# Factors by root and reciprocal, the skip in the segment's number, whole-block searches, and earlier norms of heads in a graph-attention kernel

## The chip, the cores and the metric

The kernel runs on one core of one Trainium2 chip. The metric is the device time in microseconds. Before the change the median of three runs is 234.67 us (234.59 to 234.72). Beside them stands one profiled execution of 234.5 us, whose recorded span is 233.0 us.

## The reference

One layer of graph attention over 4096 nodes with 512 features and 4 heads, a residual, and a layer norm:

```python
ht = (h @ W).reshape(N, 4, 512).transpose(1, 0, 2)
src, dst = einsum('hnd,hd->hn', ht, a_src), einsum('hnd,hd->hn', ht, a_dst)
e = leaky_relu(src[:, :, None] + dst[:, None, :], 0.01) + adj[None]
att = softmax(e, axis=-1)
x = layernorm(x + einsum('hij,hjd->hid', att, ht).mean(axis=0))   # eps 1e-5
```

Here h is x (4096x512, fp32), adj is 4096x4096 in fp32, W is 512x2048 and a holds two vectors of 512 for each head. The entries of adj are zero, or positive numbers up to 1e9. The scores from src and dst are small beside them, so in a row whose two largest entries lie far enough apart the softmax is one at the largest entry, in all four heads. Then the row of the attention result is x at that column, times the mean of the four W.

## The kernel before, in words

The kernel works by that. For each row it finds the column of the largest entry of adj, gathers the row of x of that column (y), multiplies it by the mean of the heads' W (w_sum), adds the row's own x, and normalises. In the end it tests for each row, with bounds from the norms of W, a and x, that the second largest entry is far enough below. Only where a row fails does a general path run (the function general).

The rows are cut into 32 blocks of 128. The main loop runs over turns t = 0 to 31. All engines take their instructions in the order in which the program lists them, since the schedule is written out by hand (manual_schedule). A turn works on several blocks at once:

- SyncE issues the load of the adj tile of block t + 5 (2 MB, a ring of six tiles; it waits until the search of block t - 1 has let go of its tile) and, every fourth turn, a load of rows of x.
- VectorE searches tile t (segment_maxima: the largest entry of each segment of 16, 32 or 64 columns, in two halves of 2048 columns; then find_segment: the largest of these and its index), and finds the column of block t - 2 (find_column). In most turns up to 19 (the tuple END) the column comes after the segment, later between the two halves of the search.
- GpSimd computes the row numbers for an indirect gather of the winning segment (fetch_segment, tile lead) and for the gather of the rows of x (gather_rows, tile y).
- TensorE transposes the gathered rows of block t - 3 (turn) and multiplies them by w_sum (products). For blocks 1 to 17 (TABLED) rows of x below number 128 are not gathered. GpSimd adds SKIP (8192) to their number, which puts it out of bounds, the gather leaves the cleared tile as it is, and the row comes from a small table through a one-hot matrix (spread, from_table).
- ScalarE makes that one-hot matrix (Square, then Relu), copies the transposed rows (yt), sums squares of W and x, and takes the mean and the sum of squared deviations of block t - 4 (parked_stats, at the end of its turn); it applies the norm of block t - 9 (finish).

Every fourth turn from 8 to 28, rstd turns four blocks' sums into factors 1/sqrt(var + eps). In the kernel before GpSimd does all of it: a scaling, a power with exponent -0.5, a product for the shift and a scaling. GpSimd's order in such a turn is: row and lead of block t, then the column and the gather of block t - 2, then rstd. head_norms has three parts, in turns 24, 26 and 28; its middle part is the first Sqrt on ScalarE.

Lines that matter: segment_maxima L196 to L206, find_segment L208, fetch_segment L216, gather_rows L236, find_column L259, spread L322, parked_stats L359, rstd L365, finish L372, head_norms L453, and the loop L523 to L584, with this in it:

```python
COLUMN, PROJECT, STATS, FINISH = 2, 3, 4, 8
END = (*range(1, 3), *range(5, 20))
...
    if t >= FINISH and t % Q == 0:
        rstd(slice(t - FINISH, t - FINISH + Q))
```

Behind the loop the last blocks are projected and normalised, the norms and the test are completed, and the finished rows are stored.

Of the kernel before, what the change touches and what calls it, by code (L numbers as in the profile page):

```python
# [9 lines left out]
F32 = mybir.dt.float32  # L10
BF16 = mybir.dt.bfloat16
U32 = mybir.dt.uint32
I32 = mybir.dt.int32
AF = mybir.ActivationFunctionType
OP = mybir.AluOpType
# [3 lines left out]
EPS = 1e-5  # L19
LOWEST = -3.4028234663852886e38  # L20
HINTED = tuple(getattr(mybir.EngineType, name) for name in ("PE", "Activation", "DVE", "Pool"))
P = 128
# [6 lines left out]
SKIP = 8192  # L29
# [43 lines left out]
def leading_rows(ctx, tc, x, adj, W, a, out, ident, n_bad, any_bad):  # L73
# [8 lines left out]
    nc = tc.nc  # L82
# [35 lines left out]
    def pieces(ib):  # L118
        return PIECES if ib == NB - 1 else 2 if ib >= LATE else 1
# [45 lines left out]
    width = once.tile([P, len(spans)], U32, name="width")  # L165
    for k, (e, _, _) in enumerate(spans):
        nc.gpsimd.iota(width[:, k : k + 1], pattern=[[0, 1]], base=e, channel_multiplier=0)
    power = once.tile([P, 4], F32, name="power")
    nc.gpsimd.memset(power, -0.5)
    eps = once.tile([P, 1], F32, name="eps")  # L170
    nc.gpsimd.memset(eps, EPS)
    zero = once.tile([P, 1], F32, name="zero")
    nc.gpsimd.memset(zero, 0.0)
    nth = once.tile([P, 1], I32, name="nth")
    nc.gpsimd.iota(nth, pattern=[[0, 1]], base=0, channel_multiplier=-1)
    minus = once.tile([P, 1], F32, name="minus")
    nc.gpsimd.tensor_copy(minus, nth)
    ident_b = once.tile([P, P], BF16, name="ident_b")
# [17 lines left out]
    def segment_maxima(ib, lo, hi):  # L196

        e = spans[span_of(ib)][0]
        if lo == 0:
            seg_of[ib] = small.tile([P, N // e], F32, name=f"seg{e}", bufs=2)  # L200
        n = max(pieces(ib), 2)
        for k in range(lo * n // PIECES, hi * n // PIECES):
            nc.vector.tensor_reduce(  # L203
                seg_of[ib][:, ts(k, N // e // n)],
                adj_t[ib][:, ts(k, N // n)].rearrange("p (s e) -> p s e", e=e), axis=AX.X, op=OP.max,
            )  # L206
# [9 lines left out]
    def fetch_segment(ib):  # L216
        at = at_of.pop(ib)
        row = small.tile([P, 1], U32, name="row")
        nc.gpsimd.tensor_tensor(row, at[:, 0:1], first[:, ib : ib + 1], op=OP.add)  # L219
        k = span_of(ib)  # L220
        e = spans[k][0]
        lead = lead_pool.tile([P, e], F32, name=f"lead{e}", bufs=LEADS[k])
        nc.gpsimd.indirect_dma_start(  # L223
            out=lead, out_offset=None, in_=adj_segs[e],
            in_offset=bass.IndirectOffsetOnAxis(ap=row[:, :1], axis=0),
        )
        lead_of[ib] = lead
        if ib < NB - 1:
            start = at_of[ib] = small.tile([P, 1], U32, name="start")
            nc.gpsimd.tensor_tensor(start, at[:, 0:1], width[:, k : k + 1], op=OP.mult)  # L230

    def clear_rows(ib):
        y = y_t[ib] = y_pool.tile([P, D], F32, name="y")
# [2 lines left out]
    def gather_rows(ib, col):  # L236
        if ib not in TABLED:
            y = y_t[ib] = y_pool.tile([P, D], F32, name="y")
            nc.gpsimd.indirect_dma_start(  # L239
                out=y, out_offset=None, in_=x,  # L240
                in_offset=bass.IndirectOffsetOnAxis(ap=col[:, :1], axis=0),
            )
            return
        away = small.tile([P, 1], U32, name="away")
        nc.gpsimd.tensor_scalar(away, col, float(P), float(SKIP), op0=OP.is_lt, op1=OP.mult)
        there = small.tile([P, 1], U32, name="there")
        nc.gpsimd.tensor_tensor(there, col, away, op=OP.add)  # L247
        nc.gpsimd.indirect_dma_start(  # L248
            out=y_t[ib], out_offset=None, in_=x,
            in_offset=bass.IndirectOffsetOnAxis(ap=there[:, :1], axis=0),  # L250
            bounds_check=N - 1, oob_is_err=False,
        )
        low = low_of[ib] = small.tile([P, 1], BF16, name="low")
        nc.gpsimd.tensor_scalar(low, col, float(P), None, op0=OP.min)

    def find_inner(ib):
        nc.vector.max(out=inner[:, ib, :], in_=lead_of[ib])
# [94 lines left out]
    def stats(ib):  # L352
        o, i = o_ps[ib], slice(ib, ib + 1)
        sq = rows.tile([P, D], F32, name="sq")
        nc.scalar.activation(sq, o, AF.Identity, scale=-1.0 / D, accum_out=nm[:, i])
        sq = rows.tile([P, D], F32, name="sq")
        nc.scalar.activation(sq, o, AF.Square, bias=nm[:, i], accum_out=sd[:, i])

    def parked_stats(ib):  # L359
        o, i = o_ps.pop(ib), slice(ib, ib + 1)  # L360
        nc.scalar.activation(hold[:, ib, :], o, AF.Identity, scale=-1.0 / D, accum_out=nm[:, i])  # L361
        sq = rows.tile([P, D], F32, name="sq")
        nc.scalar.activation(sq, hold[:, ib, :], AF.Square, bias=nm[:, i], scale=-float(D), accum_out=sd[:, i])  # L363

    def rstd(i):  # L365
        nc.gpsimd.tensor_scalar(sd[:, i], sd[:, i], 1.0 / D, EPS, op0=OP.mult, op1=OP.add)
        nc.gpsimd.tensor_tensor(sd[:, i], sd[:, i], power[:, : i.stop - i.start], op=OP.pow)  # L367
        nc.gpsimd.tensor_mul(nm[:, i], nm[:, i], sd[:, i])
        if i.stop <= BEHIND:
            nc.gpsimd.tensor_scalar(sd[:, i], sd[:, i], -float(D), None, op0=OP.mult)  # L370
# [82 lines left out]
    def head_norms(part):  # L453

        if part == 0:
            each = once.tile([2 * H, 2 * H], F32, name="each")
            nc.vector.tensor_scalar_mul(each, ident[: 2 * H, : 2 * H], aa)
            pw = of_norms[0] = psum.tile([P, KB * H + 2 * H], F32, name="px", bufs=1)
            nc.tensor.matmul(pw[:, : KB * H], ones, ww, start=True, stop=True)
            nc.tensor.matmul(pw[:, KB * H :], ones[: 2 * H, :], each, start=True, stop=True)  # L460
        elif part == 1:
            pw = of_norms[0]
            w2 = once.tile([P, H], F32, name="w2")
            nc.vector.tensor_reduce(
                w2, pw[:, : KB * H].rearrange("p (k h) -> p h k", h=H), axis=AX.X, op=OP.add
            )
            for s in range(2):
                nc.vector.tensor_mul(n2[:, ts(s, H)], pw[:, ds(KB * H + s * H, H)], w2)
            nc.scalar.activation(n2, n2, AF.Sqrt)
        else:  # L470
            both = once.tile([P, H], F32, name="both")
            nc.vector.tensor_add(both, n2[:, :H], n2[:, H:])
            nc.vector.tensor_reduce(vn, both, axis=AX.X, op=OP.max)
# [44 lines left out]
    squares = list(range(KB * H))  # L518
    squares_at = {t: 2 if t < 7 else 1 for t in range(3, 15)}
    COLUMN, PROJECT, STATS, FINISH = 2, 3, 4, 8  # L520
    END = (*range(1, 3), *range(5, 20))

    for t in range(NB):  # L523
        if t == NB // 2:
            tc.mark_branch_hint_location("general", engines=HINTED)
        if t in x_at:
            load_x(*x_at[t])
        if t + AHEAD == NB - 1:
            load_x(LATE, Q)
        load_adj(t + AHEAD)  # L530
        middle = 1 if t == NB - 1 else 2
        segment_maxima(t, 0, middle)
        if t >= COLUMN and t not in END and t != COLUMN + 1:
            find_column(t - COLUMN)
        segment_maxima(t, middle, PIECES)
        if t == NB - 1:
            for ib in (BEHIND, BEHIND + 2):
                load_x(ib, 2)
        find_segment(t)
        if t in END:  # L540
            find_column(t - 1 if t <= COLUMN else t - COLUMN)
        if t + 1 in TABLED:
            clear_rows(t + 1)
        if t >= FINISH and t % Q == 0:
            rstd(slice(t - FINISH, t - FINISH + Q))
        if t < 2:
            mean_of_heads(t)
        elif t == 2:
            mean_of_heads(2)
            mean_of_heads(3)  # L550
            fill_table()
        if t == 0:
            square_sums_of_a()
        if t in (24, 26, 28):
            head_norms((t - 24) // 2)
        ib = t - PROJECT
        if t == NB - 1:
            for late in range(LATE, NB):
                row_norm(late)
        if t == NB - 2:  # L560
            residual(LATE)
            residual(LATE + 1)
        if ib >= 0:
            if ib in TABLED:
                spread(ib)
            turn(ib)
            if ib > BEHIND:
                products(ib - 1, KB - 1, KB)
            if ib < BEHIND:
                residual(ib)  # L570
            if ib in TABLED:
                from_table(ib)
            products(ib, 0, KB if ib < BEHIND else KB - 1)
            if ib == 0:
                split_table()
        for _ in range(squares_at.get(t, 0)):
            square_sum_of_w(squares.pop(0))
        if t >= BEHIND + STATS:
            put_by(t - STATS)
        elif t >= STATS:  # L580
            row_norm(t - STATS)
            parked_stats(t - STATS)
        if t > FINISH:
            finish(t - FINISH - 1)  # L584

# [32 lines left out]
    test()  # L618
    turn(NB - 2)
    stats(BEHIND + 2)  # L620
    rstd(slice(BEHIND, BEHIND + 3))
    products(NB - 3, KB - 1, KB)
    pg = count()
# [209 lines left out]
```

## Time and profile before

| | |
|---|---|
| median of three runs | 234.67 us |
| profiled execution, time and span | 234.5 us, 233.0 us |
| TensorE busy | 194.3 us (83%) |
| VectorE busy | 191.1 us (82%) |
| ScalarE busy | 139.8 us (60%) |
| GpSimd busy | 112.9 us (48%) |
| DMA | 96.45 MB, 414 GB/s in the mean |
| chain that ended last | DMA 64%, VectorE 19%, TensorE 6% |

Times in the profile are in us and counted from the start of the span; durations in the tables of groups are in ns. DVE is VectorE, ACT is ScalarE, PE is TensorE, POOL is GpSimd, SP is SyncE; L203 is line 203 of the kernel. A group is named by what it writes and reads (seg<-adj_t). In brackets, or behind an arrow, stands how long the engine sat idle before an instruction and what ended that. In order of time, neighbouring instructions of one line are joined ("x2"). PEclk is the clock that TensorE was granted, as a share of full speed.

### The profile page before, as it was taken

What the parts mean: (1) busy time and instruction counts of PE and PEld (TensorE: products, weight loads), DVE (VectorE), ACT (ScalarE), POOL (GpSimd) and SP (SyncE); (2) the same over time, 40 slices, a digit from 0 to 9 for tenths busy, and PEclk for the clock granted to TensorE, in tenths of its full rate; (3) what the DMA queues carried; (4) which work ended last, traced back from release to release, by engine and by line L of the source; (5) the groups of instructions that cost most, each with busy time, mean ns of one, the idle gap of its engine ahead of it and who ended that gap; (6) DMA issues with size and microseconds to landing.
All of it is one profiled execution on the core that took longest, in us unless ns stands there. A gap on an engine that the chain in (4) does not pass through costs nothing.

```text
span 233.0 us, 2399 instructions
## 1 busy us (share of the span) xinstructions
PE 194.3 (83%) x570; PEld 92.6 (40%) x576; DVE 191.1 (82%) x301; ACT 139.8 (60%) x340; POOL 112.9 (48%) x260
## 2 busy tenths in 40 slices
PE   0069988789099996999899999999999977899990
PEld 0024443334044443445344444544443433345460
DVE  0448299899969997999799958977999999988782
ACT  3002213588077775699798767767756763289761
POOL 4020415615554875467657755653465447557210
PEclk9999999999769998899999999999999999999998
DMA  6999999999999999999999999999999999999985
GB/s 229 433 422 437 420 437 421 438 427 414 436 431 420 422 433 434 427 421 434 423 426 424 432 429 427 420 430 430 429 432 413 427 422 425 410 425 418 424 357 203
DMA packets 12834, 96.45 MB, mean 414 GB/s; under 512 B 2087, under 2 KB 2535, under 8 KB 7056
## 3 DMA queue, kind: packets, MB, share of 16 engines
q1 hardware_dynamic: 9216, 88.08, 89.5%
q0 software_dynamic: 3584, 8.16, 8.9%
q8 instruction: 5, 0.08, 0.1%
q14 instruction: 13, 0.11, 0.1%
q10 hardware_dynamic: 16, 0.02, 0.0%
HBM read 88.54 MB, written 8.39 MB: 416 GB/s over the span
## 4 chain that ended last, share of the span: by engine, by line
DMA 64%; DVE 19%; PE 6%; ACT 4%; issue 3%; POOL 1%; SPq 0%; DVEq 0%; POOLq 0%
DMA adj_t<-in_adj_dram 56%; DVE seg L203 16%; DMA hold<-in_L_gnn_W_dram 5%; PE o L296 4%; DMA y<-in_x_dram,col 3%; ACT sq L340 2%; PE o L384 2%; DVE at L212 1%; ACT hold L375 1%; DVE top L210 1%; PE tp L277 1%; DVE within L263 1%; POOL sd L367 0%; POOL lead L223 0%; ACT yt L279 0%
## 5 line engine op out<-in xcount | busy, mean ns | idle before, releaser
L203 DVE TENSOR_REDUCE seg<-adj_t 128x128 f32<-128x2048 f32 (+3 forms) x66 | 144.1, 2210 | 29.8 <-DMA adj_t<-in_adj_dram 29.7
L296 PE MATMUL o<-w_sum,yt 128*128 128x512 f32 x248 | 114.4, 602 | 2.0 <-ACT yt L279 1.8
L296 PEld LDWEIGHTS o<-w_sum,yt 128*128 128x128 f32 x248 | 46.3, 193 | 54.9 <-issue 42.6
L279 ACT COPY yt<-tp 128x512 f32<-128x512 f32 x33 | 19.1, 579 | 34.3 <-PE tp L277 34.3
L223 POOL DMA_INDIRECT lead<-in_adj_dram,row x32 | 32.6, 1020 | 13.1 <-POOL row L219 13.1
L277 PE MATMUL tp<-ident,y 128*128 128x128 f32 x128 | 22.5, 300 | 15.9 <-DMA y<-in_x_dram,there 12.0
L219 POOL TENSOR_TENSOR row<-at,first 128x1 uint32<-128x1 uint32 x32 | 6.1, 191 | 54.0 <-DVE at L212 45.4
L277 PEld LDWEIGHTS tp<-ident,y 128*128 128x128 f32 x128 | 18.7, 208 | 30.5 <-issue 27.0
L435 PE MATMUL o<-hold,ident 128*128 128x512 f32 x32 | 17.0, 699 | 13.7 <-DMA hold<-in_L_gnn_W_dram 13.7
L289 PE MATMUL o<-hold,ident 128*128 128x512 f32 x52 | 27.5, 614 | 0.0
L248 POOL DMA_INDIRECT y<-in_x_dram,there x17 | 18.9, 1111 | 10.9 <-POOL there L247 5.6
L340 ACT ACTIVATE sq<-hold 128x512 f32<-128x512 f32 x32 | 19.9, 624 | 0.0
L375 ACT ACTIVATE hold<-hold,nm,sd 128x512 f32<-128x512 f32 x24 | 19.1, 802 | 0.0
L239 POOL DMA_INDIRECT y<-in_x_dram,col x15 | 14.9, 995 | 7.6 <-POOL col L265 7.0
L363 ACT ACTIVATE sq<-hold,nm 128x512 f32<-128x512 f32 x24 | 17.4, 724 | 0.8
L435 PEld LDWEIGHTS o<-hold,ident 128*128 128x128 f32 x32 | 7.1, 226 | 22.8 <-issue 22.3
L436 ACT ACTIVATE w_sum<-o 128x512 f32<-128x512 f32 x4 | 2.4, 597 | 22.9 <-PE o L435 22.9
L326 ACT ACTIVATE off<-px,minus 128x128 f32<-128x128 f32 x17 | 6.3, 368 | 15.3 <-PE px L324 15.3
L361 ACT ACTIVATE hold<-o 128x512 f32<-128x512 f32 x24 | 14.3, 597 | 0.8
L336 PE MATMUL o<-z,pick 128*128 128x512 bf16 x46 | 13.9, 407 | 0.2
L210 DVE MAX8 top<-seg 128x8 f32<-128x256 f32 (+2 forms) x32 | 11.6, 361 | 1.1
L212 DVE FIND_INDEX8 at<-top,seg 128x8 uint32<-128x256 f32 (+2 forms) x32 | 11.3, 352 | 0.0
(113 smaller groups left out, 178.7 us busy)
## 6 DMA issues: line engine op xcount, KB each, us to landing
adj_t<-in_adj_dram SPq DMA_DIRECT2D x28, 2048.0 KB, 33.0
hold<-in_x_dram SPq DMA_DIRECT2D x6, 1024.0 KB, 32.4
adj_t<-in_adj_dram SPq DMA_DIRECT2D x6, 1024.0 KB, 28.1
hold<-in_L_gnn_W_dram SPq DMA_DIRECT2D x2, 2048.0 KB, 16.6
out_dram<-hold SPq DMA_DIRECT2D x7, 512.0 KB, 5.4
out_dram<-hold SPq DMA_DIRECT2D x3, 1024.0 KB, 15.1
adj_t<-in_adj_dram SPq DMA_DIRECT2D x4, 512.0 KB, 19.8
hold<-in_x_dram SPq DMA_DIRECT2D x2, 512.0 KB, 14.4
```

Source lines behind the costliest of these rows:

```text
L203: nc.vector.tensor_reduce(seg_of[ib][:, ts(k, N // e // n)], adj_t[ib][:, ts(k, N // n)].rearrange("p (s e) -> p s e", e=e), axis=AX.X, op ...
L223: nc.gpsimd.indirect_dma_start(out=lead, out_offset=None, in_=adj_segs[e], in_offset=bass.IndirectOffsetOnAxis(ap=row[:, :1], axis=0),)
L239: nc.gpsimd.indirect_dma_start(out=y, out_offset=None, in_=x, in_offset=bass.IndirectOffsetOnAxis(ap=col[:, :1], axis=0),)
L248: nc.gpsimd.indirect_dma_start(out=y_t[ib], out_offset=None, in_=x, in_offset=bass.IndirectOffsetOnAxis(ap=there[:, :1], axis=0), bounds_c ...
L277: nc.tensor.transpose(tp[:, kb, :], y[:, ds(kb, P, KB)], ident)
L279: nc.scalar.copy(yt, tp)
L289: nc.tensor.matmul(o_ps[ib], ident, hold[:, ib, :], start=start, stop=False)
L296: nc.tensor.matmul(o_ps[ib], yt_of[ib][:, kb, :], w_sum[:, kb, :], start=(start and kb == 0), stop=(kb == KB - 1),)
L340: nc.scalar.activation(sq, hold[:, ib, :], AF.Square, accum_out=xx[:, ib : ib + 1])
L363: nc.scalar.activation(sq, hold[:, ib, :], AF.Square, bias=nm[:, i], scale=-float(D), accum_out=sd[:, i])
L375: nc.scalar.activation(hold[:, ib, :], o, AF.Identity, bias=nm[:, i], scale=sd[:, i])
L435: nc.tensor.matmul(o, ident, hold[:, w_at + kb * H + h, :], start=(h == 0), stop=(h == H - 1))
```

## The change

Four things change.

- rstd: ScalarE takes the square root of var + eps (root), VectorE the reciprocal; the product and the last scaling stay with GpSimd. root stands at the end of ScalarE's turns 7, 11, 15, 19, 23 and 27, the reciprocal in the next turn, where the whole of rstd stood. For the last three blocks before the final four both stand together behind the loop.
- The skip of the table is added where the segment's number becomes the column at which it starts (fetch_segment), by two instructions for TABLED blocks; gather_rows uses the column as it is. The number for the one-hot matrix is formed from the shifted column.
- END reaches to turn 27, and in its turns the tile is searched in one instruction over 4096 columns. So in turns 20 to 27 the column is found after the segment, too.
- The three parts of head_norms come in turns 21, 22 and 23.

```diff
-    power = once.tile([P, 4], F32, name="power")
-    nc.gpsimd.memset(power, -0.5)
...
-    nc.gpsimd.iota(nth, pattern=[[0, 1]], base=0, channel_multiplier=-1)
+    nc.gpsimd.iota(nth, pattern=[[0, 1]], base=-1, channel_multiplier=-1)
...
-        n = max(pieces(ib), 2)
+        n = max(pieces(ib), 1 if ib in END else 2)
...
-            nc.gpsimd.tensor_tensor(start, at[:, 0:1], width[:, k : k + 1], op=OP.mult)
+            if ib in TABLED:
+                away = small.tile([P, 1], F32, name="away")
+                nc.gpsimd.tensor_scalar(away, at[:, 0:1], float(P // e), float(SKIP), op0=OP.is_lt, op1=OP.mult)
+                nc.gpsimd.tensor_scalar(start, at[:, 0:1], float(e), away, op0=OP.mult, op1=OP.add)
+            else:
+                nc.gpsimd.tensor_tensor(start, at[:, 0:1], width[:, k : k + 1], op=OP.mult)
...
-        away = small.tile([P, 1], U32, name="away")
-        nc.gpsimd.tensor_scalar(away, col, float(P), float(SKIP), op0=OP.is_lt, op1=OP.mult)
-        there = small.tile([P, 1], U32, name="there")
-        nc.gpsimd.tensor_tensor(there, col, away, op=OP.add)
         nc.gpsimd.indirect_dma_start(
             out=y_t[ib], out_offset=None, in_=x,
-            in_offset=bass.IndirectOffsetOnAxis(ap=there[:, :1], axis=0),
+            in_offset=bass.IndirectOffsetOnAxis(ap=col[:, :1], axis=0),
             bounds_check=N - 1, oob_is_err=False,
         )
-        nc.gpsimd.tensor_scalar(low, col, float(P), None, op0=OP.min)
+        nc.gpsimd.tensor_scalar(low, col, float(SKIP - 1), float(SKIP - 1), op0=OP.max, op1=OP.subtract)
...
+    def root(i):
+        nc.scalar.activation(sd[:, i], sd[:, i], AF.Sqrt, bias=eps, scale=1.0 / D)
+
     def rstd(i):
-        nc.gpsimd.tensor_scalar(sd[:, i], sd[:, i], 1.0 / D, EPS, op0=OP.mult, op1=OP.add)
-        nc.gpsimd.tensor_tensor(sd[:, i], sd[:, i], power[:, : i.stop - i.start], op=OP.pow)
+        nc.vector.reciprocal(sd[:, i], sd[:, i])
         nc.gpsimd.tensor_mul(nm[:, i], nm[:, i], sd[:, i])
...
-    END = (*range(1, 3), *range(5, 20))
+    END = (*range(1, 3), *range(5, 28))
...
-        middle = 1 if t == NB - 1 else 2
+        middle = PIECES if t in END else 1 if t == NB - 1 else 2
         segment_maxima(t, 0, middle)
         if t >= COLUMN and t not in END and t != COLUMN + 1:
             find_column(t - COLUMN)
-        segment_maxima(t, middle, PIECES)
+        if t not in END:
+            segment_maxima(t, middle, PIECES)
...
-        if t in (24, 26, 28):
-            head_norms((t - 24) // 2)
+        if 21 <= t < 24:
+            head_norms(t - 21)
...
             parked_stats(t - STATS)
+        if FINISH <= t + 1 < NB and (t + 1) % Q == 0:
+            root(slice(t + 1 - FINISH, t + 1 - FINISH + Q))
         if t > FINISH:
             finish(t - FINISH - 1)
...
     stats(BEHIND + 2)
+    root(slice(BEHIND, BEHIND + 3))
     rstd(slice(BEHIND, BEHIND + 3))
```

## The prediction

> **What bounds the kernel now.** I read the page's head first, then the waits of VectorE, then VectorE and ScalarE in order of time.
>
> ```profile
> span 233.0 us, 2399 instructions
> DMA  6999999999999999999999999999999999999985
> ```
>
> From its second slice the DMA row is full: 4096x4096 numbers come in as 32 tiles, one per turn. VectorE searches each tile as it lands, so the next question is how much it has to spare. This is its waits between 72 and 200 us (total us, times, longest):
>
> ```profile
> DVE seg L203 <- DMA adj_t<-in_adj_dram: 8.5, 7, 2.7
> ```
>
> VectorE has 8.5 us of slack over turns 9 to 28, about 0.4 a turn, and no other entry stands in that answer: today it waits for nothing but tiles. It is the second bound, close behind the first. Its last instruction of a turn, and the first of the next, in order of time (start, duration):
>
> ```profile
> 71.91 0.17 DVE L263 FIND_INDEX8 within<-top,lead 128x8 uint32<-128x16 f32 x1
> 72.00 4.46 DVE L203 TENSOR_REDUCE seg<-adj_t 128x128 f32<-128x2048 f32 x2
> 77.66 4.46 DVE L203 TENSOR_REDUCE seg<-adj_t 128x128 f32<-128x2048 f32 x2
> ...
> 95.90 0.17 DVE L263 FIND_INDEX8 within<-top,lead 128x8 uint32<-128x16 f32 x1
> 95.98 4.46 DVE L203 TENSOR_REDUCE seg<-adj_t 128x128 f32<-128x2048 f32 x2
> ...
> 119.81 0.17 DVE L263 FIND_INDEX8 within<-top,lead 128x8 uint32<-128x16 f32 x1
> ...
> 143.96 0.28 DVE L212 FIND_INDEX8 at<-top,seg 128x8 uint32<-128x128 f32 x1
> ...
> 169.44 0.28 DVE L212 FIND_INDEX8 at<-top,seg 128x8 uint32<-128x128 f32 x1
> ...
> 191.56 0.22 DVE L212 FIND_INDEX8 at<-top,seg 128x8 uint32<-128x64 f32 x1
> 191.95 2.28 DVE L203 TENSOR_REDUCE seg<-adj_t 128x32 f32<-128x2048 f32 x1
> ```
>
> These are the ends of turns 8, 12, 16, 20, 24 and 28, the six turns in which the loop calls rstd. A turn without a wait takes 77.66 - 72.00 = 5.66 us. Now ScalarE's last instruction of the statistics in turns 7, 11, 15, 19, 23 and 27, which is what rstd needs (with three other rows that I use below):
>
> ```profile
> 75.10 0.19 ACT L363 ACTIVATION_READ_ACCUMULATOR sq<-hold,nm 128x1 f32 x1
> ...
> 94.21 0.18 ACT L363 ACTIVATION_READ_ACCUMULATOR sq<-hold,nm 128x1 f32 x1
> ...
> 101.50 0.18 ACT L363 ACTIVATION_READ_ACCUMULATOR sq<-hold,nm 128x1 f32 x1
> ...
> 124.34 0.19 ACT L363 ACTIVATION_READ_ACCUMULATOR sq<-hold,nm 128x1 f32 x1
> ...
> 147.16 0.19 ACT L363 ACTIVATION_READ_ACCUMULATOR sq<-hold,nm 128x1 f32 x1
> ...
> 162.89 0.19 ACT L363 ACTIVATION_READ_ACCUMULATOR sq<-hold,nm 128x1 f32 x1
> ...
> 167.73 0.18 ACT L363 ACTIVATION_READ_ACCUMULATOR sq<-hold,nm 128x1 f32 x1
> ...
> 180.18 1.28 ACT L469 ACT_TABLE_LOAD   x1
> ...
> 189.76 0.19 ACT L363 ACTIVATION_READ_ACCUMULATOR sq<-hold,nm 128x1 f32 x1
> ```
>
> Set against each other: in turn 8 VectorE is through at 72.08 and the statistics of the turn before at 75.29; in turn 12 it is 96.07 against 101.68; in turn 16 119.98 against 124.53; in turn 20 144.24 against 147.35. ScalarE ends turn t-1 three to five and a half us after VectorE has ended turn t. Only in turns 24 (169.72 against 167.91) and 28 (191.78 against 189.95) is it ahead. Before, GpSimd bore this wait, after its gather of the turn, where it harmed little:
>
> ```profile
> 99.32 1.12 POOL L248 DMA_INDIRECT y<-in_x_dram,there  x1 [0.68 <-ACT yt L279]
> ...
> 101.77 0.19 POOL L366 TENSOR_SCALAR sd<-sd 128x4 f32<-128x4 f32 x1 [1.04 <-ACT sq L363]
> ...
> 214.31 0.96 POOL L239 DMA_INDIRECT y<-in_x_dram,col  x1 [0.61 <-PE tp L277]
> ```
>
> **The change part by part.** The small terms first. These are the groups by shape (busy us, mean ns):
>
> ```profile
> L203 DVE TENSOR_REDUCE seg<-adj_t 128x128 f32<-128x2048 f32 x36 | 80.5, 2277 | 23.6 <-DMA adj_t<-in_adj_dram 23.6
> L203 DVE TENSOR_REDUCE seg<-adj_t 128x16 f32<-128x1024 f32 x4 | 4.7, 1204 | 0.0
> L245 POOL TENSOR_SCALAR away<-col 128x1 uint32<-128x1 uint32 x17 | 4.2, 246 | 1.5
> L367 POOL TENSOR_TENSOR sd<-sd,power 128x4 f32<-128x4 f32 x6 | 6.3, 1051 | 0.5
> L401 ACT ACTIVATE sd<-mv,eps 128x1 f32<-128x1 f32 x5 | 1.4, 287 | 1.6 <-DVE mv L399 1.6
> L404 DVE RECIPROCAL sd<-sd 128x1 f32<-128x1 f32 x5 | 0.8, 156 | 0.8 <-ACT sd L401 0.7
> ```
>
> Whole-block search. 1024 more elements cost 2277 - 1204 = 1073 ns, so 4096 in one instruction take 2277 + 2146 = 4423 ns, where the pair takes 4460 by the clock (4.46). Gain 0.04 us a block, bounds 0 and 2 x 2277 - 4423 = 131 ns; over 25 blocks 1 us, 0 to 3.3. I use 5.6 us for a turn. In turns 20 to 27 the column is now found after the segment, so those gathers go out half a search later; that is counted below.
>
> Skip by segment. Two small GpSimd instructions and their hand-overs leave the way from column to gather, one is added ahead of it. The added forms have no row; by L245's 246 ns for a near one the gather goes out 0.3 us sooner (bounds 0 and 0.7). Its low is one instruction as before.
>
> Norms of heads in 21 to 23. The same instructions elsewhere. VectorE's few tenths of them move from turns 24, 26, 28 to three turns that the wait below covers; I put 0.4 us there.
>
> Factors. GpSimd loses the power (1051 ns) and the scaling. ScalarE gets one Sqrt of 128x4 every fourth turn, near L401's 287 ns, VectorE one reciprocal near L404's 156 ns. The table load of 1.28 us now comes with the first Sqrt, in turn 7; it was the one of turn 26, so none is added. Ahead of the price of these instructions goes their order: the reciprocal stands in VectorE's queue of turn t, behind find_column(t-2) and ahead of the search of t+1, and it waits for a Sqrt that stands at the end of ScalarE's turn t-1. By the pairs above VectorE then stands still. Behind it are queued all further searches, and through them every column, gather, transpose and release of a tile.
>
> One sentence from outside the trace: the Trainium skill (ScalarE: Activation LUTs, What ACT_TABLE_LOAD costs) adds to a load of 1283 ns a drain of about 1380 ns; our load is the 1.28 us above, and by the page the first stall, and the total, would be up to 1.4 us longer.
>
> **What a stall costs.** Write R(t) for the moment VectorE gets past the reciprocal of turn t. First, R(8): statistics at 75.29, less the 0.3 of the earlier gather, load 1.28, root 0.28, reciprocal 0.16, two hand-overs of 0.05: 76.8, where the next search began at 72.00. So 4.8 us late. The delay does not stay there, because ScalarE itself depends on VectorE: the last statistics that R(t+4) needs are of block t-1, in turn t+3; they come behind the projection of block t in that turn, whose rows are gathered when turn t+2 has found its columns. The way from there:
>
> ```profile
> 90.25 0.72 PE L277 MATMUL tp<-ident,y 128*128 128x128 f32 x4 [1.90 <-DMA y<-in_x_dram,there]
> ...
> 159.63 0.63 PE L277 MATMUL tp<-ident,y 128*128 128x128 f32 x4
> ...
> 164.47 0.63 PE L277 MATMUL tp<-ident,y 128*128 128x128 f32 x4
> ...
> 222.24 0.63 PE L277 MATMUL tp<-ident,y 128*128 128x128 f32 x4
> ```
>
> Column to gather 99.32 - 96.07 = 3.25, less 0.3, is 2.95. Gather to landing is this (of L248, then of L239):
>
> ```profile
> DMA to landing us min/median/max: 7.2/8.3/9.2
> ```
>
> ```profile
> DMA to landing us min/median/max: 6.1/7.2/8.8
> ```
>
> so 8.3. Transposes to the end of the statistics 94.39 - 90.25 = 4.14. Root, reciprocal and hand-overs 0.54. Together 15.9 us after the end of turn t+2, which itself is two turns after R(t): R(t+4) = R(t) + 11.2 + 15.9 = R(t) + 27.1, where the tiles now allow 4 x (5.66 + 0.4), about 24. One more term is TensorE's clock. Between R(t) and the next rows it now runs dry for some 5 us, and these windows (length, busy, granted clock) show a turn behind a gap of 1.90 us against one without:
>
> ```profile
> 90.25:97.44 7.19, 7.19 (x17) 0.76 1.01 428
> 97.44:102.97 5.53, 5.53 (x19) 1.00 1.01 430
> ```
>
> The turn behind the gap starts at R + 5.6 + 2.95 + 8.3 = R + 16.85 and with 7.2 us ends at R + 24.05, while the next rows are there at R + 22.45: 1.6 us more, 28.7 in all. (Bounds 0 and 1.6; I take the upper, since the gap is longer than the one in the row. The Trainium skill, TensorE: Matmul & The Clock Gate, What's actually happening, halves the clock after an idle window of about 3.4 us: with gaps of 5 us it too speaks for the longer one, though our row shows 0.76 behind only 1.90.)
>
> Hence R(12) = 76.8 + 28.7 = 105.5. From turn 15 the squares of W are gone from ScalarE's turn, some 0.7: R(16) = 133.5; with turns 18 and 19 a little shorter R(20) = 161.2. Then the blocks without the table: two turns and the head norms 11.2, column to gather 2.5, landing 7.2, transposes to statistics 163.08 - 159.63 = 3.45, 0.54, and behind the gap a turn of 4.84 (164.47 - 159.63) drawn out by 7.19/5.53, 0.6 to 0.8 late: 25.5 and 25.3, so R(24) = 186.7 and R(28) = 212.0. Before, the search of turn 29 began at 191.95: 20.05 us late. Today the last gather (214.31 + 7.2 = 221.5) meets a TensorE that is busy until 222.24; that 0.7 is given back. Span 233.0 + 20.05 - 0.7 = 252.3; the profiled execution took 234.5 for its span of 233.0, so 253.8. That execution lies 0.17 below the median of 234.67, which I leave out.
>
> The tiles don't limit this. From issue to landing a tile takes, in the page's DMA issues (count, KB, median us):
>
> ```profile
> adj_t<-in_adj_dram SPq DMA_DIRECT2D x28, 2048.0 KB, 33.0
> ```
>
> So 33 us of loads stand ahead of it, and 20 us of lateness does not empty that queue; the 8.5 us of VectorE's slack are what the sum has already used up.
>
> Own range of the forecast: with TensorE always at full clock 6.2 us less, 247.6; with each of the six gathers at its fastest (1.1 less) 247.2, at its slowest (0.9 to 1.6 more) up to 261. Both at once are unlikely.
>
> **The rivals.**
>
> The lateness is taken up. If ScalarE's times stayed as they are (TensorE working off a backlog, not waiting for new rows), R(12) would be 102.1, R(16) 125, R(20) 148, and from there slack brings VectorE back: about 234.5, no change. For it: only some turns of TensorE wait for a gather today. Against: the row at 90.25 waits 1.90 us for exactly such rows, and a VectorE that is 5 us later leaves no backlog. A half of it, one or two stalls paid, ends near 240.
>
> Faster. ScalarE is early enough and no reciprocal waits. Then the 1.05 us power and its neighbours leave GpSimd's turn 28, which lies on the chain of waits ahead of a late gather, and the time is 234.5 - 1.3 - about 0.7 for the searches = 232.5. It decides where the statistics end before VectorE's turn; in four of six pairs above they don't.
>
> The table is loaded again and again. If Relu (the pick of turns 4 to 20) were not served by the table that Sqrt brings, each root up to turn 19 would cost two loads, about 2.6 us in R(12), R(16), R(20): near 260. No load follows the one at 180.18, behind which Square, Identity and Copy run, but no Relu does. (The Trainium skill, ScalarE: Activation LUTs, Table sets: the hidden batching unit, has the cheap functions in every set, which speaks against it.)
>
> **How the numbers follow.** The forecast has 0.80, half taken up 0.06, the table again 0.04, fully taken up 0.04, faster 0.06. 245 to 259 holds the forecast but for its corners, so about 8 in 10. What a measurement here can tell is about 0.2%, 0.5 us. Slower 0.80 + 0.06 + 0.04 = 0.90; same 0.04; faster 0.06.
>
> **What would show it.** VectorE's waits would have a new row, its reciprocal of sd waiting for ScalarE's sd, six times and 25 to 32 us in total, 4 to 6.5 each in turns 8 to 20; its wait for tiles between 72 and 200 us would be near nothing. TensorE's clock row would show dips behind each stall. The searches would be one instruction near 4.42 us, 25 of them; one table load stands in turn 7. The forecast is wrong if that wait is under 10 us in total, if tile waits remain beside it, or if later stalls shrink from turn to turn.

## The result, and the profile after

The changed kernel takes 255.5 us in the median (254.38 to 256.49, 4 runs), beside 234.63 us for the kernel before (4 runs): 1.089 times as long, 95% interval 1.0843 to 1.0941. 253.8 us had been forecast. The profiled execution took 254.38 us for a span of 252.8 us. Two of the kernels below have runs more than 1.5% above their fastest one, at a lower mean clock of TensorE; the ratios leave such runs out.

The head of its page:

```profile
span 252.8 us, 2358 instructions
...
PEclk9999999998699977999799989999799889999996
DMA  6999999999999999999999999999999999725144
GB/s 240 434 428 439 424 424 432 425 419 438 424 438 411 438 429 425 419 437 427 432 425 435 420 431 424 420 444 418 421 422 427 415 423 410 259 86 217 37 168 170
```

DMA keeps its rate up to some 215 us, and then falls to 37 to 259 GB/s: the tiles are in, and the engines are not through with them. TensorE's clock row has dips that recur. VectorE's waits between 72 and 230 us (us in total, times, longest):

```profile
DVE sd L368 <- ACT sd L365: 27.7, 6, 6.7
DVE at L210 <- issue: 0.7, 2, 0.4
```

The wait for tiles, 8.5 us before in the window up to 200 us, is gone, and the reciprocal of sd (L368) waits 27.7 us for ScalarE's Sqrt (L365). Its six places in VectorE's order of time, with the search behind each:

```profile
76.64 0.18 DVE L368 RECIPROCAL sd<-sd 128x4 f32<-128x4 f32 x1 [4.19 <-ACT sd L365]
76.73 4.39 DVE L201 TENSOR_REDUCE seg<-adj_t 128x256 f32<-128x4096 f32 x1
...
105.86 0.18 DVE L368 RECIPROCAL sd<-sd 128x4 f32<-128x4 f32 x1 [6.65 <-ACT sd L365]
105.95 4.39 DVE L201 TENSOR_REDUCE seg<-adj_t 128x256 f32<-128x4096 f32 x1
...
133.49 0.18 DVE L368 RECIPROCAL sd<-sd 128x4 f32<-128x4 f32 x1 [5.07 <-ACT sd L365]
...
160.45 0.18 DVE L368 RECIPROCAL sd<-sd 128x4 f32<-128x4 f32 x1 [5.16 <-ACT sd L365]
...
186.77 0.18 DVE L368 RECIPROCAL sd<-sd 128x4 f32<-128x4 f32 x1 [3.65 <-ACT sd L365]
...
210.98 0.18 DVE L368 RECIPROCAL sd<-sd 128x4 f32<-128x4 f32 x1 [3.00 <-ACT sd L365]
211.07 2.25 DVE L201 TENSOR_REDUCE seg<-adj_t 128x32 f32<-128x2048 f32 x1
```

The search of turn 29 starts at 211.07 us and started at 191.95 before: 19.1 of the 19.8 us that the span grew are there by then. The table load stands in turn 7, right ahead of the first Sqrt; apart from the load at the start of the kernel it is the only one:

```profile
74.81 0.18 ACT L362 ACTIVATION_READ_ACCUMULATOR sq<-hold,nm 128x1 f32 x1
75.02 1.28 ACT L365 ACT_TABLE_LOAD   x1
76.31 0.30 ACT L365 ACTIVATE sd<-sd,eps 128x4 f32<-128x4 f32 x1
```

### The profile page after: what moved, and what is told of

It is laid out like the page before. It is cut to its first block, busy times and chain, and to the rows that moved or that the text cites. A ratio compares the mean times of both kernels' runs of the same rounds, so it can differ in the third digit from the quotient of the medians.

```text
span 252.8 us, 2358 instructions
## 1 busy us (share of the span) xinstructions
PE 200.2 (79%) x570; PEld 95.9 (38%) x576; DVE 189.4 (75%) x283; ACT 141.9 (56%) x347; POOL 101.4 (40%) x228
## 4 chain that ended last, share of the span: by engine, by line
DMA 36%; PE 21%; DVE 14%; ACT 13%; issue 8%; POOL 6%; SPq 0%; POOLq 0%; DVEq 0%
DMA y<-in_x_dram,col 18%; DMA adj_t<-in_adj_dram 13%; PE o L295 12%; DVE seg L201 9%; DMA hold<-in_L_gnn_W_dram 5%; PE o L288 4%; PE tp L276 3%; POOL lead L221 3%; ACT sq L339 3%; ACT sq L362 2%; ACT yt L278 2%; PE o L335 1%; ACT hold L360 1%; ACT hold L376 1%; DVE at L210 1%
## 5 line engine op out<-in xcount | busy, mean ns | idle before, releaser
L201 DVE TENSOR_REDUCE seg<-adj_t 128x256 f32<-128x4096 f32 (+4 forms) x41 | 141.8, 3467 | 21.5 <-DMA adj_t<-in_adj_dram 21.5
L295 PEld LDWEIGHTS o<-w_sum,yt 128*128 128x128 f32 x248 | 47.0, 195 | 56.2 <-issue 44.2
L278 ACT COPY yt<-tp 128x512 f32<-128x512 f32 x33 | 19.1, 579 | 49.3 <-PE tp L276 49.3
L276 PE MATMUL tp<-ident,y 128*128 128x128 f32 x128 | 24.2, 317 | 27.7 <-DMA y<-in_x_dram,col 27.7
L276 PEld LDWEIGHTS tp<-ident,y 128*128 128x128 f32 x128 | 19.5, 209 | 41.6 <-issue 38.0
L288 PE MATMUL o<-hold,ident 128*128 128x512 f32 x52 | 31.8, 701 | 0.0
L436 PE MATMUL o<-hold,ident 128*128 128x512 f32 x32 | 17.0, 697 | 13.7 <-DMA hold<-in_L_gnn_W_dram 13.7
L368 DVE RECIPROCAL sd<-sd 128x4 f32<-128x4 f32 (+1 forms) x7 | 1.2, 178 | 29.4 <-ACT sd L365 29.4
L247 POOL DMA_INDIRECT y<-in_x_dram,col x17 | 18.3, 1076 | 5.2 <-POOL col L264 4.6
L376 ACT ACTIVATE hold<-hold,nm,sd 128x512 f32<-128x512 f32 x24 | 19.1, 802 | 0.0
L242 POOL DMA_INDIRECT y<-in_x_dram,col x15 | 14.6, 971 | 5.2 <-POOL col L264 4.6
L437 ACT ACTIVATE w_sum<-o 128x512 f32<-128x512 f32 x4 | 2.4, 597 | 22.8 <-PE o L436 22.8
```

The lines of the kernel that those rows point to most:

```text
L201: nc.vector.tensor_reduce(seg_of[ib][:, ts(k, N // e // n)], adj_t[ib][:, ts(k, N // n)].rearrange("p (s e) -> p s e", e=e), axis=AX.X, op ...
L247: nc.gpsimd.indirect_dma_start(out=y_t[ib], out_offset=None, in_=x, in_offset=bass.IndirectOffsetOnAxis(ap=col[:, :1], axis=0), bounds_che ...
L276: nc.tensor.transpose(tp[:, kb, :], y[:, ds(kb, P, KB)], ident)
L278: nc.scalar.copy(yt, tp)
L288: nc.tensor.matmul(o_ps[ib], ident, hold[:, ib, :], start=start, stop=False)
L295: nc.tensor.matmul(o_ps[ib], yt_of[ib][:, kb, :], w_sum[:, kb, :], start=(start and kb == 0), stop=(kb == KB - 1),)
```

## The experiments

Some are the changed kernel with a part undone or shifted, some the kernel before with a part alone. Ratios are to the kernel before on the same chip.

**The power brought back.** From the changed kernel:

```diff
+        nc.gpsimd.tensor_scalar(sd[:, i], sd[:, i], 1.0 / D, EPS, op0=OP.mult, op1=OP.add)
+        nc.gpsimd.tensor_tensor(sd[:, i], sd[:, i], power[:, : i.stop - i.start], op=OP.pow)
-        nc.vector.reciprocal(sd[:, i], sd[:, i])
...
-        if FINISH <= t + 1 < NB and (t + 1) % Q == 0:
-            root(slice(t + 1 - FINISH, t + 1 - FINISH + Q))
...
-    root(slice(BEHIND, BEHIND + 3))
```

> The changed kernel with the factors computed as before: GpSimd's scaling and power come back, Sqrt and reciprocal go; the skip, the whole-block search, the later columns of turns 20 to 27 and the earlier norms of heads stay. Theory (the whole loss is VectorE waiting for ScalarE's Sqrt): no wait of VectorE for sd is left in the loop and the time is 233 to 235 us. Rival (the columns found after the segment in turns 20 to 27, or the search in one piece, make gathers late): at least some 3 us of the loss stay, 238 us or more.

235.64 us, ratio 1.005 (1.0014 to 1.0087). VectorE's waits between 72 and 200 us hold no Sqrt and the old slack again:

```profile
DVE seg L203 <- DMA adj_t<-in_adj_dram: 7.6, 5, 2.5
```

So without the factors nearly all of the loss is gone; but 1.2 us stay, less than the rival's 3 and more than the theory allowed.

**The factors alone.** To the kernel before:

```diff
+    def root(i):
+        nc.scalar.activation(sd[:, i], sd[:, i], AF.Sqrt, bias=eps, scale=1.0 / D)
...
-        nc.gpsimd.tensor_scalar(sd[:, i], sd[:, i], 1.0 / D, EPS, op0=OP.mult, op1=OP.add)
-        nc.gpsimd.tensor_tensor(sd[:, i], sd[:, i], power[:, : i.stop - i.start], op=OP.pow)
+        nc.vector.reciprocal(sd[:, i], sd[:, i])
...
+        if FINISH <= t + 1 < NB and (t + 1) % Q == 0:
+            root(slice(t + 1 - FINISH, t + 1 - FINISH + Q))
...
+    root(slice(BEHIND, BEHIND + 3))
```

> The kernel before with the factors alone changed (Sqrt on ScalarE at the end of turn t-1, reciprocal on VectorE in turn t). Theory: the recurrence with a turn of 5.66 us and the gather 0.3 us later gives periods near 29 us up to turn 20; in turns 20 to 27 the column is found between the halves, some 2.5 us sooner, which shortens the last two periods by about that: 250 to 257 us, VectorE's wait for the Sqrt 22 to 32 us in the loop. Rival (the loss needs the other parts as well): under 245 us.

251.26 us, ratio 1.0708 (1.0661 to 1.0754), as the theory had it. The reciprocals in VectorE's order of time:

```profile
77.82 0.18 DVE L367 RECIPROCAL sd<-sd 128x4 f32<-128x4 f32 x1 [5.96 <-ACT sd L364]
107.22 0.18 DVE L367 RECIPROCAL sd<-sd 128x4 f32<-128x4 f32 x1 [6.60 <-ACT sd L364]
136.59 0.18 DVE L367 RECIPROCAL sd<-sd 128x4 f32<-128x4 f32 x1 [6.56 <-ACT sd L364]
165.13 0.18 DVE L367 RECIPROCAL sd<-sd 128x4 f32<-128x4 f32 x1 [6.58 <-ACT sd L364]
186.64 0.16 DVE L367 RECIPROCAL sd<-sd 128x4 f32<-128x4 f32 x1
208.46 0.16 DVE L367 RECIPROCAL sd<-sd 128x4 f32<-128x4 f32 x1
```

Periods of 29.40, 29.37 and 28.54 us, where some 29 had been worked out, and then no wait at all in turns 24 and 28. There the column is still found between the halves of the search, so the rows can be gathered sooner, and the Sqrt is early enough. The last two stalls of the changed kernel thus need another part of the change as well. The columns behind the segment in turns 20 to 27 fit; no run put them alone beside the factors.

**The same instructions a turn later.** From the changed kernel:

```diff
-        if t >= FINISH and t % Q == 0:
-            rstd(slice(t - FINISH, t - FINISH + Q))
+        if t > FINISH and t % Q == 1:
+            rstd(slice(t - 1 - FINISH, t - 1 - FINISH + Q))
```

> The changed kernel with rstd called in turns 9, 13, 17, 21, 25 and 29 instead of 8 to 28: the same instructions on the same engines, the reciprocal one turn behind the Sqrt. Theory: the Sqrt ends near 76.6 and 102 us where VectorE ends turns 9 and 13 at 77.6 and 101.6, so at most half a us of wait is left in each of the six, and with the 8.5 us of slack the time is 233 to 236 us. Rival (it is the table load, the Sqrt on ScalarE or the reciprocal itself that costs): still over 245 us.

237.79 us, ratio 1.0133 (1.0111 to 1.0156). Sqrt, reciprocal and table load are all there, the loop has no wait for the Sqrt any more, and 17.7 of the 20.9 us are gone. So it is the place of the wait, not the instructions. VectorE between 72 and 215 us:

```profile
DVE seg L201 <- DMA adj_t<-in_adj_dram: 8.3, 7, 2.3
```

But the time lies above the 236 us of the expectation: 3.3 us remain. The next runs take that up.

**The Sqrt made later.** To the changed kernel, ahead of each root in the loop:

```diff
+            for _ in range(4):
+                nc.scalar.copy(rows.tile([P, D], F32, name="sq"), zero.to_broadcast([P, D]))
             root(slice(t + 1 - FINISH, t + 1 - FINISH + Q))
```

> The changed kernel with four extra copies of 512 numbers to a scratch tile on ScalarE ahead of each of the six roots in the loop, together about 2.1 us, so that each Sqrt ends that much later. Theory (the loop closes on itself, nothing takes up the delay): each of the six periods grows by the whole 2.1 us, 12 to 13 us in all, 266 to 269 us. Rival (the stall is partly slack that a later Sqrt uses up, or lateness is made up between two stalls): under 262 us.

264.17 us in the median of four runs, but they lie apart: one at 260.0 and three from 263.93 to 264.74. That is 4.5 us above the changed kernel for the shortest and 8.4 to 9.2 for the others. None reaches the theory's 266, and the shortest lies in the rival's range; one run is too few to say how much of the delay is paid. The profiled execution is one of the three longer ones (264.42). Its reciprocals:

```profile
78.98 0.18 DVE L368 RECIPROCAL sd<-sd 128x4 f32<-128x4 f32 x1 [6.84 <-ACT sd L365]
110.26 0.18 DVE L368 RECIPROCAL sd<-sd 128x4 f32<-128x4 f32 x1 [8.71 <-ACT sd L365]
141.09 0.18 DVE L368 RECIPROCAL sd<-sd 128x4 f32<-128x4 f32 x1 [8.26 <-ACT sd L365]
171.57 0.18 DVE L368 RECIPROCAL sd<-sd 128x4 f32<-128x4 f32 x1 [8.69 <-ACT sd L365]
195.56 0.18 DVE L368 RECIPROCAL sd<-sd 128x4 f32<-128x4 f32 x1 [1.30 <-ACT sd L365]
222.24 0.18 DVE L368 RECIPROCAL sd<-sd 128x4 f32<-128x4 f32 x1 [5.48 <-ACT sd L365]
```

In this execution nothing takes up the delay up to turn 20: the periods are 31.28, 30.83 and 30.48 us, 2.1, 3.2 and 3.5 above the changed kernel's 29.22, 27.63 and 26.96. Then one period has only 23.99 instead of 26.32. VectorE is 26.8 us late by then (its search starts at 171.67, at 144.87 before), and the window behind it (length; busy of TensorE, its weight loads, VectorE, ScalarE, GpSimd; clock, DMA share, GB/s) shows that DMA has no load left to do for 5 us:

```profile
172.00:177.00 5.00, 4.91 (x14) 1.93 (x13) 4.86 (x7) 4.11 (x11) 0.34 (x3) 1.00 0.00 0
```

The first gather behind R(20), where R(t) is again the moment VectorE gets past the reciprocal of turn t, and the transposes that wait for its rows, in the changed kernel and then here:

```profile
168.17 0.95 POOL L242 DMA_INDIRECT y<-in_x_dram,col  x1 [0.27 <-POOL col L264]
176.44 0.96 PE L276 MATMUL tp<-ident,y 128*128 128x128 f32 x4 [3.27 <-DMA y<-in_x_dram,col]
```

```profile
179.30 0.95 POOL L242 DMA_INDIRECT y<-in_x_dram,col  x1 [0.27 <-POOL col L264]
184.16 0.72 PE L276 MATMUL tp<-ident,y 128*128 128x128 f32 x4 [1.45 <-DMA y<-in_x_dram,col]
```

From the gather to the transposes it takes 4.9 us instead of 8.3. With that TensorE's gap is 1.45 us and not 3.27, and its clock over the 5.5 us behind it 1.00 and not 0.69. So the shorter period comes with rows that land sooner behind the empty queue, and with the full clock that follows.

**TensorE kept busy in the gap.** To the changed kernel, at the end of TensorE's turns 9, 13 and 17, matmuls into a spare bank that nobody reads:

```diff
+            if t in (9, 13, 17):
+                warm = psum.tile([P, P], F32, name="px", bufs=1)
+                for _ in range(24 if t < 17 else 18):
+                    nc.tensor.matmul(warm, ident, ident, start=True, stop=True)
```

> The changed kernel with 24 (turns 9 and 13) and 18 (turn 17) extra 128x128 transposing matmuls into a spare bank at the end of TensorE's turn, so that it is busy for some 3.5 and 2.6 us of the gap in which it waits for rows behind a stall. Nothing reads them. Theory (a turn behind the gap runs at a granted clock near 0.7 and takes about 2 us more, and that is on the way to the next Sqrt): the clock in those turns is near 1, the next R come about 1.6 to 2 us sooner each, 4 to 6 us in all: 249 to 252 us. Rival (the slow turn is not on that way, or the clock follows something else than idle time): 254 us or more.

253.41 us in the median of the three runs that the ratio uses (250.22 to 253.94; the fourth took 254.16), ratio 1.0734 (1.0654 to 1.0813) where the changed kernel has 1.0892. That is 2.1 us below the changed kernel by the medians and 3.7 by the ratios: faster, but by less than the theory's 4 to 6, and the median lies between the two ranges. TensorE's windows (length, busy, clock, DMA share, GB/s), the turn behind the first gap of the changed kernel and the same turn here:

```profile
93.53:101.20 7.67, 7.67 (x17) 0.69 0.99 420
```

```profile
94.48:100.01 5.53, 5.48 (x17) 1.00 1.00 423
```

The clock does follow the idle time: filled, it is 1.00 and the turn takes 5.53 instead of 7.67 us. But from one R to the next (reciprocals at 77.91, 105.22, 132.82 and 159.26) it is 27.31, 27.60 and 26.44 us against 29.22, 27.63 and 26.96: 1.9, nothing and 0.5 gained. In the first two periods TensorE then stands before rows that have not landed:

```profile
100.68 0.75 PE L276 MATMUL tp<-ident,y 128*128 128x128 f32 x4 [0.46 <-DMA y<-in_x_dram,col]
...
128.90 0.75 PE L276 MATMUL tp<-ident,y 128*128 128x128 f32 x4 [0.29 <-DMA y<-in_x_dram,col]
```

These are 22.8 and 23.7 us behind R, where I had the rows landed after 22.45. And the extra matmuls took longer than expected, 5.5 and 4.2 us and not 3.5 and 2.6, so in the second and third gap they outlast the wait. In the third:

```profile
145.50 4.18 PE L581 MATMUL px<-ident 128*128 128x128 f32 x36
149.79 0.70 PE L276 MATMUL tp<-ident,y 128*128 128x128 f32 x4
```

The transposes start behind them without a wait, 17.0 us after R, in the changed kernel 15.8; in the second gap it is 17.7 against 16.8. So the run shows that the clock costs time, but the 0 and 0.5 are not its whole price.

**What remains without the stalls.** Each other part alone on the kernel before. The search in one piece and the columns behind the segment up to turn 27:

```diff
-    END = (*range(1, 3), *range(5, 20))
+    END = (*range(1, 3), *range(5, 28))
...
-        n = max(pieces(ib), 2)
+        n = max(pieces(ib), 1 if ib in END else 2)
...
-        middle = 1 if t == NB - 1 else 2
+        middle = PIECES if t in END else 1 if t == NB - 1 else 2
...
```

> The kernel before with END up to turn 27 and the search in one piece as the only change. Theory for the 1.2 us that were left with the power brought back: the columns of turns 20 to 27 come half a search later, TensorE runs dry once more (2.8 us at 174 us in that run) and reaches the end with more work left: slower by 1 to 1.5 us. Rival (it comes from the norms or the skip): within 0.5 us of before, or faster by the 1 us that the searches save.

236.42 us, ratio 1.0086 (1.0056 to 1.0115): slower by 1.9 us, a little more than the theory's 1 to 1.5. TensorE's order of time shows the late column, and the backlog that it leaves to the end:

```profile
174.76 0.72 PE L277 MATMUL tp<-ident,y 128*128 128x128 f32 x4 [3.25 <-DMA y<-in_x_dram,col]
...
224.19 0.63 PE L277 MATMUL tp<-ident,y 128*128 128x128 f32 x4
```

The last transposes start at 224.19, at 222.24 before.

The skip in the segment's number:

```diff
...
+                nc.gpsimd.tensor_scalar(away, at[:, 0:1], float(P // e), float(SKIP), op0=OP.is_lt, op1=OP.mult)
+                nc.gpsimd.tensor_scalar(start, at[:, 0:1], float(e), away, op0=OP.mult, op1=OP.add)
...
-        nc.gpsimd.tensor_scalar(away, col, float(P), float(SKIP), op0=OP.is_lt, op1=OP.mult)
-        nc.gpsimd.tensor_tensor(there, col, away, op=OP.add)
...
```

> The kernel before with the skip added in the segment's number as the only change. Theory: the gather of blocks 1 to 17 goes out 0.3 to 0.7 us sooner, which TensorE's few waits for it before 150 us can use, but the end is set by TensorE's work after 200 us: no change, within 0.5 us of before. Rival (the second instruction with a column as its scalar costs more than the two that go): slower by 0.5 us or more.

234.59 us, ratio 1.0001 (0.9983 to 1.002): no change.

The norms of heads in turns 21 to 23:

```diff
-        if t in (24, 26, 28):
-            head_norms((t - 24) // 2)
+        if 21 <= t < 24:
+            head_norms(t - 21)
```

> The kernel before with the norms of heads in turns 21 to 23 as the only change. Theory: some 0.7 us of VectorE's work and one table load move into turns in which VectorE has slack before the next tile: within 0.5 us of before. Rival (the second part, one turn after the first instead of two, makes VectorE wait for TensorE): slower by more than 0.5 us, and a wait of VectorE for px in the loop.

234.38 us, ratio 0.9986 (0.9968 to 1.0003): no change that can be told, and no new wait of VectorE in the loop.

Sqrt and reciprocal for the last three blocks behind the loop:

```diff
+        if i.stop <= BEHIND:
...
+        else:
+            nc.scalar.activation(sd[:, i], sd[:, i], AF.Sqrt, bias=eps, scale=1.0 / D)
+            nc.vector.reciprocal(sd[:, i], sd[:, i])
```

> The kernel before with Sqrt on ScalarE and reciprocal on VectorE only for the last three blocks behind the loop; the loop keeps the power on GpSimd. Theory: VectorE waits some 1.7 us for that Sqrt, as in the run with rstd a turn later, while the last blocks' moments stand behind it; that sets the end back by 0.7 to 1.5 us: 235.2 to 236 us. Rival (the end is set by TensorE, the wait is covered): within 0.5 us of before.

234.59 us, ratio 1.0005 (0.9986 to 1.0024). VectorE does wait there, by its waits:

```profile
DVE sd L371 <- ACT sd L370: 1.7, 1, 1.7
```

but the time doesn't show it: the rival was right. So of the 3.3 us of the kernel with rstd a turn later, the late columns explain up to 1.9; for the rest no single part was found, and its cause stays open.

**A version without stalls and late columns.** From the changed kernel: rstd a turn later in the loop, the power on GpSimd for the last three blocks, END back to turn 19.

> The changed kernel with three edits: rstd a turn later (9 to 29) in the loop, the factors of the last three blocks on GpSimd by power as before, END back to turn 19. Theory: no wait for the Sqrt, no late columns, and GpSimd's 1.9 us of rstd in turn 28 no longer stand ahead of the gather that TensorE waits for at 203 us: 233 to 234.5 us, at most 1 us faster than before. Rival (the earlier norms or the Sqrt's place cost something): 235 us or more.

234.53 us, ratio 0.9994 (0.9973 to 1.0015): as fast as before and no faster, so the gain of up to 1 us that the theory allowed isn't there. No version was found that beats the kernel before.

## Why the prediction was right, and where it was off

**The order of the queues** was right, and it is shown: the factors alone make 1.0708, without them 1.005 is left, and the same instructions a turn later have no wait in the loop. The pairs of times that the prediction set against each other are what decides.

**The recurrence** was right to within a us at each step: R was forecast at 76.8, 105.5, 133.5, 161.2, 186.7 and 212.0 us, and the searches behind the six reciprocals start at 76.73, 105.95, 133.58, 160.54, 186.87 and 211.07. The waits add up to 27.7 us (25 to 32 forecast). The single waits fall from 6.65 us in turn 12 to 3.00 in turn 28, as the forecast's periods do (28.7 to 25.3), but no stall makes up for an earlier one: against the kernel before, the searches behind the six reciprocals are 4.7, 10.0, 13.7, 15.7, 17.1 and 19.1 us late. The rival of lateness taken up would have had this shrink.

**The term of TensorE's clock** was near its size, though the run that was to test it can't show that. It stood in the sum with 1.6 us in each of the first three periods, 4.8 together. In the changed kernel the second gather behind R(8), its landing and the transposes of its rows are:

```profile
90.82 1.08 POOL L247 DMA_INDIRECT y<-in_x_dram,col  x1 [0.27 <-POOL col L264]
```

```profile
DMA to landing us min/median/max: 8.4/8.4/8.4
```

```profile
101.31 0.70 PE L276 MATMUL tp<-ident,y 128*128 128x128 f32 x4
```

The rows are there at 99.2 us, 22.6 behind R (22.45 forecast), and TensorE comes to them 2.1 us later, since the turn before was drawn out. In the next two periods the rows land at 128.6 and 155.0 us (issue at 120.05 and 146.82, 8.6 and 8.1 us to landing) and the transposes start at 129.56 and 156.51: 0.9 and 1.6 later. That is 4.6 together. Filling the gaps gave back 1.9, 0 and 0.5: in the second period of that run the rows themselves came as late as 23.7 us behind R, and the extra matmuls outlast the second and third gap.

The Trainium skill (TensorE: Matmul & The Clock Gate, What's actually happening) was weighed there for the longer turn, and for the clock itself the trace agrees: 0.69 behind a gap of 5.25 us and 1.00 with the gap filled; only its idle window of about 3.4 us is no lower limit here, where the clock was 0.76 behind 1.90 us.

**The table load** cost what its row says. The Sqrt starts 0.01 us behind the end of the load, and the load 0.03 us behind the instruction before it, so the drain of about 1.4 us that the Trainium skill (ScalarE: Activation LUTs, What ACT_TABLE_LOAD costs) adds is not in this trace. The rival of repeated loads falls: Relu runs in turns 8 to 20 behind the load at 75.02 without another; there the Trainium skill (ScalarE: Activation LUTs, Table sets: the hidden batching unit) was right.

**The small parts.** The one-piece search takes 4405 ns (4423 forecast):

```profile
L201 DVE TENSOR_REDUCE seg<-adj_t 128x256 f32<-128x4096 f32 x15 | 66.1, 4405 | 12.2 <-DMA adj_t<-in_adj_dram 12.2
```

The gather goes out 2.87 us behind the column (forecast 2.95), the norms are free. Here the prediction failed in one step: it booked the search in one piece as a gain of 1 us and the later columns only inside the periods. Alone, the two together cost 1.9 us: the late rows make TensorE run dry once more, for 3.25 us, and its last transposes start 1.95 us later than before. In the changed kernel it can't be told apart from the stalls; with the stalls gone it remains.

**The end.** From the search of turn 29 to ScalarE's last instruction it takes 36.9 us (before 37.3, and 0.7 less was forecast); then 4.9 us to the end of the span, before 3.7. The sum came out at 252.3 for a span of 252.8, and that close by luck: R(28) was 0.9 too late and this end 1.4 too short. What makes the last stretch longer was not tried.

## What to carry to other kernels

An instruction that costs 0.18 us is not cheap in a queue whose owner is ahead of the engine it waits for: before a step is moved to another engine, set the end of its input against the time at which that queue gets there, turn by turn. If the input itself comes from that queue a fixed number of turns earlier, the stall does not wear off but sets the period of the loop: turns in between times their length, plus the way round. One turn of distance more was enough to take the wait out of the loop here.

## What the runs showed of the hardware that was not expected

How short a gap slows TensorE down. Behind a gap of 1.13 us its granted clock stayed at 1.00 in the kernel before, behind one of 5.25 us it was 0.69 in the changed kernel:

```profile
115.39 0.72 PE L277 MATMUL tp<-ident,y 128*128 128x128 f32 x4 [1.13 <-DMA y<-in_x_dram,there]
```

```profile
115.39:120.89 5.50, 5.50 (x17) 1.00 1.00 419
```

```profile
93.53 1.10 PE L276 MATMUL tp<-ident,y 128*128 128x128 f32 x4 [5.25 <-DMA y<-in_x_dram,col]
```

Near 2 us it goes either way: the kernel before had 0.76 over the turn behind 1.90 us. These windows of 5.5 us stand behind gaps of 2.08 us (the factors alone), 1.91 us (the Sqrt made later) and 2.29 us (the last three blocks alone):

```profile
208.71:214.21 5.50, 5.50 (x12) 0.69 1.02 421
```

```profile
80.12:85.62 5.50, 5.50 (x18) 1.00 1.04 439
```

```profile
197.93:203.43 5.50, 5.50 (x16) 1.00 1.02 415
```

So the length alone does not decide it there; what else does, no run shows. A gap of 5.25 us cost little more than the one of 1.90: the turn took 7.67 us instead of 7.19.

And the latency of a gather. With DMA full, gathers of 128 rows landed in 6.1 us at the least (the kernel before, late in its loop) and 9.7 us at the most (the changed kernel, blocks 1 to 17):

```profile
DMA to landing us min/median/max: 6.8/8.2/9.7
```

In the changed kernel, whose loads end earlier than its work, the shortest took 3.2 us:

```profile
DMA to landing us min/median/max: 3.2/6.8/8.8
```

There that comes only behind the last stall. With the Sqrt made later the queue ran dry between two stalls, and the period got shorter; a sum with one latency for all gathers does not see that.
